# Two graph layers on one core: program order in two stretches, pair projections in another order, setup in smaller pieces

## The chip, the core and the metric

One core of a Trainium2 chip runs the whole program. The time is that of the device, in microseconds (us), from the first to the last instruction of one execution, and the number compared is the median of several executions. Five engines work side by side, each through its own list of instructions in order: TensorE (PE) multiplies matrices, VectorE (DVE) and ScalarE (ACT) work elementwise and can read what TensorE left in its accumulators (PSUM, eight banks of 128 x 512 fp32), GpSimd (POOL) works elementwise on the on-chip memory (SBUF) and issues stores, and SyncE (SP) issues loads. An engine waits where an instruction needs what another has not yet finished. A tile framework puts in these waits, hands out buffers from pools, and may reorder the instructions of an engine by its own estimate of when each will be ready. `keep_in_program_order` takes that freedom from an instruction.

## The reference

Two layers of attention on a graph with 2,708 nodes and 1,024 features, all in fp32 (the biases `bf`, `bg`, `bW` exist but hold zeros):

```python
def _L0_gnn_ref(x, adj, Wf, bf, Wg, bg, W, bW):
    f = x @ Wf + bf
    g = x @ Wg + bg
    e = jax.nn.relu(f @ g.T)
    attention = jax.nn.softmax(jnp.where(adj > 0, e, NEG), axis=1)
    return attention @ (x @ W + bW)

def _L1_gnn_ref(input, adj, W, a1, a2):
    h = input @ W
    e = jax.nn.leaky_relu(h @ a1 + (h @ a2).T, negative_slope=0.2)
    attention = jax.nn.softmax(jnp.where(adj > 0, e, neg), axis=1)
    return jax.nn.relu(attention @ h)

# x: (2708, 1024), adj: (2708, 2708) int32
h = jnp.maximum(_layernorm(x), 0.0)
x = x + _L0_gnn_ref(h, adj, ...)
h = jnp.maximum(_layernorm(x), 0.0)
x = x + _L1_gnn_ref(h, adj, ...)
```

## The kernel before

The kernel works by panels of 512 or a few more columns (p = 0 to 4) and by pairs of 128-row tiles (q = 0 to 9, and one left-over pair, LEFT). Every product of 2 x 2 blocks is made from seven products instead of eight, named M1 to M7; some of the seven accumulate in the same PSUM bank, one after the other, so the bank must have been read in between.

**Stages.** First `M = Wf Wg^T`, by rows, with transposes of `Wf` and `Wg` on TensorE. Then for each panel of layer 0: `project_q` (B = M h), `scores` (h B, mask, running maximum), softmax, `aggregate` (attention times h), `project` (times W, plus x). Layer 1 has only `aggregate` and `project`. The projection of the last panel goes pair by pair (`by_pair`), so that its rows are done early.

**Work handed out behind TensorE.** Small pieces of vector work wait in a list; `behind(us)` is called after each product and spends a credit on them. The loads of the first two entries are issued ahead.

```python
def one():
    for it in later[:2]:
        if it[1]:
            it[1]()
            it[1] = None
    us, _, go = later.pop(0)[:3]
    go()
    return us

def behind(us, psum_free=False):
    credit[0] = min(credit[0] + us, 2 * us)
    while later and credit[0] > 0 and (psum_free or not later[0][3]) and (...):
        credit[0] -= one()
```

**The setup of the pairs.** For each pair of row tiles: load x, layernorm (`norms`), store the rows, transpose them on TensorE (`transposes`, needs a PSUM bank), form the sums of the seven products (`sums`) and store them in `hs_d`, from which `scores` loads them again; and two dot products per tile (`dots`).

```python
put_norms = lambda q: put(4.2, lambda: norms(q), lambda: fetch(q))
put_rows = lambda q: put(0.5, lambda: rows(q))
put_dots = lambda q: put(3.2, lambda: bias(q), ready=lambda: vb[0] is not None)
...
transposed_wg(0, ws)                 # 32 transposes into 8 banks, copied out by DVE and ACT in turn
for a in range(NC):
    ...
        transposed_wf(i)
    half_row_of_M(a, 0)
    ...                              # a == NH: ws = fetch_wg(1); a == NH + 2: transposed_wg(1, ws)
    bias_of_g(a, ws)
    behind(2.0 if a < NH else 5.0, True)
```

**Scores.** TensorE makes seven products per pair; DVE adds and masks them; `make_until(q + 2)` forces the setup of the pairs two ahead.

```python
rate = (0.6, 1.0, 0.65, 0.65, 0.65)[p]
...
nc.hold = True                       # DVE in program order from here
for q in range(NQ):
    make_until(q + 2)
    if q + 2 <= LEFT:
        fetch(q + 2)                 # adjacency for the masks
    ...
    product(q, M1, X, True)          # each loads As <- hs_d, then 4 matmuls
    ...
    behind(rate, True)               # after each product
```

**Projection.** `finish` adds a product to the rows of x and stores them; `join` adds a term that two outputs share.

```python
ws = {m: load_W(l, m) for m in (M1, M2)}
lefts = []
for ta, tb, (a11, a12), (a21, a22) in todo:      # four DVE sums per pair, all pairs first
    s = [slot(f"ps{i}", (P, NH, P)) for i in range(4)]
    add(s[0], a21, a22); sub(s[1], s[0], a11); sub(s[2], a11, a21); sub(s[3], a12, s[1])
    lefts.append({M1: a11, M2: a12, M5: s[0], M6: s[1], M7: s[2], M3: s[3], M4: a22})
...
copy1 = nc.vector.tensor_copy if by_pair and l == 0 else nc.scalar.copy
for group, left in (zip([[t] for t in todo], [[t] for t in lefts]) if by_pair else [(todo, lefts)]):
    for m in (M1, M2, M5, M6, M3, M7, M4):
        which = "x" if m in (M1, M2) else "y" if m in (M5, M3) else "z"      # the PSUM bank
        for i, (ta, tb, _, _) in enumerate(group):
            ...                                   # NH matmuls 128 x 512 into that bank
            if m == M1:
                copy1(t(M1), ps)
            elif m == M2:
                finish(ta, 0, ps)
            ...
            behind(rate)
```

Of the kernel before, what the change touches and what calls it, by code (L numbers as in the profile page):

```python
# [33 lines left out]
class InOrder:  # L34


    class Engine:
        def __init__(self, owner, engine):
            self.owner, self.engine = owner, engine

        def __getattr__(self, name):
            f = getattr(self.engine, name)

            def issue(*a, **k):
                i = f(*a, **k)  # L45
                return self.owner.tc.keep_in_program_order(i) if self.owner.hold else i
            return issue

    def __init__(self, tc):
        self.tc, self.nc, self.hold = tc, tc.nc, False  # L50
        self.vector = self.Engine(self, tc.nc.vector)

# [5 lines left out]
def kernel(  # L58
# [122 lines left out]

    later, credit = [], [0.0]

    def put(us, go, fetch=None, takes_psum=False, ready=None):
        later.append([us, fetch, go, takes_psum, ready])

    def one():
        for it in later[:2]:
            if it[1]:
                it[1]()  # L190
                it[1] = None
# [3 lines that stand above are left out]
# [124 lines left out]
    def make_pairs():  # L319
# [7 lines left out]

        def norms(q):
            for k in range(2):
                normalize(xs[q][k])  # L330

        def rows(q):
# [38 lines left out]

        def dots(q):
            for k, t in enumerate(units[q]):
                c = col_of[t]
                dot(r_[:, c:c + 1], xs[q][k], [vb[e][:, :W] for e in range(2)], c0)
                if t == MONO:
                    nc.gpsimd.dma_start(r_[:NM, HALF:HALF + 1], r_[NM:, c:c + 1])

        def drop(q, what):
            seen.setdefault(q, set()).add(what)  # L380
            if len(seen[q]) == 2:
                xs.pop(q)
# [5 lines left out]

        def bias(q):
            dots(q)  # L390
            drop(q, "dots")

        seen = {}
        put_norms = lambda q: put(4.2, lambda: norms(q), lambda: fetch(q))
        put_rows = lambda q: put(0.5, lambda: rows(q))
        put_dots = lambda q: put(3.2, lambda: bias(q), ready=lambda: vb[0] is not None)
        todo = [0, 1, LEFT] + list(range(2, NQ))
# [92 lines left out]
    later[0][1] = None  # L490
    bfb = row_to_all(bf, wab[0])
    transposed_wg(0, ws)
    for a in range(NC):
        for i in range(2 * a, min(2 * a + 2, NC)):
            if i + 2 < NC:
                rows_of_wf[i + 2] = load_rows(wf, i + 2, "wf")
            transposed_wf(i)
        half_row_of_M(a, 0)
        if a == NH:
            dot(c0, halves(bfb), halves(bgb))  # L500
            vb = [slot(f"vb{g}") for g in range(2)]
            for g in range(2):
                spread(vb[g][:, :W], [v[:, 4 * g + j:4 * g + j + 1] for j in range(4)])
            ws = fetch_wg(1)
        bias_of_g(a, ws)
        if a == NH + 2:
            transposed_wg(1, ws)
        behind(2.0 if a < NH else 5.0, True)
    for k in range(NH):
        for a in (k, k + NH):  # L510
            half_row_of_M(a, 1)
            wfT.pop(a)
            behind(5.5, True)
        left_of_q(k)
# [16 lines left out]

    def accumulate(left, right, K, h, order, then, evict, name, prepare={}, rate=0.0, by_k=False, more={}):

# [3 lines left out]
        for m in order:  # L537
# [4 lines left out]
            for k, d in ([(k, d) for k in range(K) for d in range(NH)] if by_k else  # L542
# [7 lines left out]
                if not by_k and k == K - 1:  # L550
                    evict[m](d, ps[d])
                    behind(rate)
            if by_k:
# [13 lines left out]
    def project_q(p, then={}):  # L567
# [55 lines left out]
        def sides(m):  # L623
            for g in range(2):
# [6 lines left out]
                else:  # L631
# [11 lines left out]
                   {M1: second, M2: fourth, M3: lambda: sides(M3), M7: lambda: sides(M7), M4: lambda: sides(M4)},  # L643
                   rate=1.2 if p == 0 else 1.5)
        return B
# [236 lines left out]
    def project(l, p, G, finish, then={}, by_pair=False, rate=2.0):  # L882
# [10 lines left out]
        start_of, join, finish = finish  # L893
        ws = {m: load_W(l, m) for m in (M1, M2)}
        start_of([t for g in todo for t in g[:2]] + ([other] if other else []))
        lefts = []
        for ta, tb, (a11, a12), (a21, a22) in todo:
            s = [slot(f"ps{i}", (P, NH, P)) for i in range(4)]
            add(s[0], a21, a22)
            sub(s[1], s[0], a11)  # L900
            sub(s[2], a11, a21)
            sub(s[3], a12, s[1])
            lefts.append({M1: a11, M2: a12, M5: s[0], M6: s[1], M7: s[2], M3: s[3], M4: a22})
        acc1 = {}
# [24 lines left out]

        copy1 = nc.vector.tensor_copy if by_pair and l == 0 else nc.scalar.copy  # L930
        for group, left in (zip([[t] for t in todo], [[t] for t in lefts]) if by_pair else [(todo, lefts)]):
            acc, tmp = {}, {}
            for m in (M1, M2, M5, M6, M3, M7, M4):
                start = m in (M1, M5, M6)
                w_ = ws.pop(m) if m in ws else load_W(l, m)
                which = "x" if m in (M1, M2) else "y" if m in (M5, M3) else "z"
                for i, (ta, tb, _, _) in enumerate(group):
# [3 lines left out]
                    for k in range(NH):  # L941
                        nc.tensor.matmul(ps, left[i][m][:, k, :], w_[k], start=(start and k == 0), stop=(k == NH - 1),  # L942
                                         skip_group_check=True)
                    if start:
                        tmp[m, i] = slot(f"pt{m}")
                    t = lambda m: tmp[m, i][:, :W]
                    o = {M3: M6, M7: M5, M4: M1}.get(m)
                    if m == M1:
                        copy1(t(M1), ps)
                    elif m == M2:  # L950
                        finish(ta, 0, ps)
                    elif o is None:
                        add(t(m), ps, t(M1))
                    elif join is None:
                        add(t(o), ps, t(o))
                        finish(tb if m != M3 else ta, 0 if m == M4 else 1, t(o))
                    else:
                        finish(tb if m != M3 else ta, 0 if m == M4 else 1, ps)
                    if join and m == M6:
                        join(tb, 1, t(M5))  # L960
# [5 lines left out]
                if m in then:  # L966
                    then.pop(m)()


# [54 lines left out]
    def scores(p, B):  # L1024
# [8 lines left out]
        S = [None] * NT  # L1033
        rate = (0.6, 1.0, 0.65, 0.65, 0.65)[p]
        lefts = {}
# [32 lines left out]

        nc.hold = True
        left_over = None  # L1070
        for q in range(NQ):
            n = P
            make_until(q + 2)
            if q + 2 <= LEFT:
                fetch(q + 2)
# [66 lines left out]
        behind(rate, True)  # L1142
        nc.hold = False
        return S, acc
# [174 lines left out]
    for p in range(NP):  # L1319
        got["S"], got["acc"] = scores(p, B)  # L1320
        generated[p] = NQ + 1
        S = got["S"]
        hooks = {M1: lambda p=p: take_max(p), M2: lambda p=p: take_softmax(p)}
        if p + 1 < NP:
            B = project_q(p + 1, hooks)
        else:
            project(0, p - 1, G.pop(p - 1), finish0(p - 1), hooks)
            scores_before()
        then = {M5: prepare_W} if p == 0 else {}
# [136 lines left out]
```

## Time and profile before

| | |
|---|---|
| time, median of 3 | 3160.89 us (3159.83 to 3162.55) |
| span of the profiled execution | 3162.6 us |
| PE busy | 3059.7 us, 97% |
| DVE, POOL, ACT busy | 1831.2, 465.2, 443.6 us |
| DMA | 651.83 MB, mean 206 GB/s |
| mean granted TensorE clock | 0.988 |

TensorE works nearly all the time, so it is read by where it does not: the table of stretches (busy time of each engine between two moments, and the TensorE clock granted there), the waits (who waited for whom, how long and how often), and the timeline (instructions of one stretch, with the idle time ahead of them in brackets). In names such as `sx<-B,As` the tile written stands left of the arrow and the tiles read right of it. Every DVE instruction bears the line of one helper, L45, so DVE's work is told apart by tiles.

### The profile page before, as it was taken

What the parts mean: (1) busy time and instruction counts of PE and PEld (TensorE: products, weight loads), DVE (VectorE), ACT (ScalarE), POOL (GpSimd) and SP (SyncE); (2) the same over time, 40 slices, a digit from 0 to 9 for tenths busy, and PEclk for the clock granted to TensorE, in tenths of its full rate; (3) what the DMA queues carried; (4) which work ended last, traced back from release to release, by engine and by line L of the source; (5) the groups of instructions that cost most, each with busy time, mean ns of one, the idle gap of its engine ahead of it and who ended that gap; (6) DMA issues with size and microseconds to landing.
All of it is one profiled execution on the core that took longest, in us unless ns stands there. A gap on an engine that the chain in (4) does not pass through costs nothing.

```text
span 3162.6 us, 36212 instructions
## 1 busy us (share of the span) xinstructions
PE 3059.7 (97%) x12712; PEld 2266.0 (72%) x12712; DVE 1831.2 (58%) x3728; ACT 443.6 (14%) x783; POOL 465.2 (15%) x664
## 2 busy tenths in 40 slices
PE   8998899999999999999999999997999999999998
PEld 5576677667876688876888885864767758678684
DVE  6767686386722687227871468558574471744612
ACT  3411020000200002001020002103131120211200
POOL 3624102110002100033000111020011020120102
PEclk9999999999999999999999999998999999999999
DMA  7878838778447795478945677686655565565655
GB/s 249 298 226 279 285 131 315 218 236 244 148 126 181 220 269 177 144 201 235 289 143 154 181 211 222 215 265 210 201 177 177 153 200 158 172 195 176 212 160 192
DMA packets 379046, 651.83 MB, mean 206 GB/s; under 512 B 170784, under 2 KB 211264, under 8 KB 378864
## 3 DMA queue, kind: packets, MB, share of 16 engines
q1 hardware_dynamic: 335920, 525.38, 55.0%
q0 software_dynamic: 42944, 124.13, 11.7%
q8 instruction: 101, 1.65, 0.2%
q14 instruction: 81, 0.66, 0.1%
HBM read 536.68 MB, written 112.67 MB: 205 GB/s over the span
## 4 chain that ended last, share of the span: by engine, by line
PE 78%; DVE 5%; DMA 3%; issue 3%; SPq 1%; POOL 0%; ACT 0%; DVEq 0%; POOLq 0%; ACTq 0%
PE gz L544 11%; PE gy L544 11%; PE gx L544 11%; PE sz L1046 6%; PE gv L544 5%; PE pz L942 5%; PE px L942 4%; PE py L942 4%; PE sx L1046 4%; PE sy L1046 4%; PE qz L544 3%; PE qy L544 2%; PE qx L544 2%; SPq L139 1%; PE po L915 1%
## 5 line engine op out<-in xcount | busy, mean ns | idle before, releaser
L1046 PE MATMUL sz<-B,As 128*128 128x288 f32 (+2 forms) x1200 | 295.3, 395 | 14.3 <-DVE st L45 10.0
L1046 PEld LDWEIGHTS sz<-B,As 128*128 128x128 f32 x1200 | 228.5, 191 | 66.1 <-DVE st L45 14.5
L850 POOL TENSOR_TENSOR gT<-gT,rr 128x2304 f32<-128x2304 f32 (+5 forms) x20 | 72.7, 3635 | 1113.3 <-DVE rr L45 1009.5
L1046 PE MATMUL sx<-B,As 128*128 128x288 f32 (+2 forms) x800 | 202.2, 396 | 18.5 <-DMA As<-hs_d 16.9
L1046 PE MATMUL sy<-B,As 128*128 128x288 f32 (+2 forms) x800 | 200.1, 393 | 3.0 <-DVE st L45 3.0
L544 PE MATMUL gz<-Sa,hc 128*128 128x288 f32 (+2 forms) x800 | 187.8, 395 | 2.3 <-ACT gT L839 2.3
L1046 PEld LDWEIGHTS sx<-B,As 128*128 128x128 f32 x800 | 152.3, 192 | 51.2 <-DMA As<-hs_d 16.7
L544 PE MATMUL gz<-P,hc 128*128 128x288 f32 (+2 forms) x800 | 186.0, 393 | 2.3 <-ACT gT L839 2.3
L544 PE MATMUL gx<-P,hc 128*128 128x288 f32 (+2 forms) x800 | 185.7, 394 | 0.0
L544 PE MATMUL gy<-T,hc 128*128 128x288 f32 (+2 forms) x800 | 184.2, 391 | 0.0
L544 PEld LDWEIGHTS gz<-Sa,hc 128*128 128x128 f32 x800 | 152.3, 191 | 37.0 <-ACT gT L839 4.8
L1046 PEld LDWEIGHTS sy<-B,As 128*128 128x128 f32 x800 | 152.3, 191 | 34.8 <-DVE st L45 4.3
L544 PEld LDWEIGHTS gz<-P,hc 128*128 128x128 f32 x800 | 150.9, 190 | 35.6 <-ACT gT L839 4.4
L544 PEld LDWEIGHTS gx<-P,hc 128*128 128x128 f32 x800 | 152.9, 191 | 32.7 <-issue 1.9
L544 PEld LDWEIGHTS gy<-T,hc 128*128 128x128 f32 x800 | 152.0, 190 | 30.5
L942 PE MATMUL px<-w,gT 128*128 128x512 f32 x320 | 147.5, 614 | 10.8 <-issue 5.8
L942 PE MATMUL py<-w,ps 128*128 128x512 f32 x320 | 141.9, 593 | 0.0
L942 PE MATMUL pz<-w,ps 128*128 128x512 f32 x320 | 141.7, 593 | 0.0
L143 POOL DMA_DIRECT2D out_dram<-x_res x180 | 89.0, 501 | 266.1 <-DVE x_res L45 230.2
L942 PEld LDWEIGHTS px<-w,gT 128*128 128x128 f32 x320 | 61.6, 196 | 88.3 <-issue 80.8
L45 DVE TENSOR_TENSOR gT<-gy,u 128x288 f32<-128x288 f32 (+2 forms) x40 | 14.8, 432 | 183.5 <-PE gy L809 183.5
L45 DVE TENSOR_TENSOR u<-gz,m 128x288 f32<-128x288 f32 (+2 forms) x40 | 17.6, 439 | 174.6 <-PE gz L544 174.2
(317 smaller groups left out, 5059.8 us busy)
## 6 DMA issues: line engine op xcount, KB each, us to landing
hc<-hg_d SPq DMA_DIRECT2D x350, 512.0 KB, 4.0
As<-hs_d SPq DMA_DIRECT2D x150, 512.0 KB, 5.0
w<-wt_d SPq DMA_DIRECT2D x96, 512.0 KB, 5.3
w<-in_L_gnn_W_dram SPq DMA_DIRECT2D x72, 512.0 KB, 3.8
md<-md_d SPq DMA_DIRECT2D x56, 512.0 KB, 4.6
adj_i<-in_adj_dram SPq DMA_DIRECT2D x200, 128.0 KB, 4.6
hg_d<-g POOLq DMA_DIRECT2D x40, 512.0 KB, 5.2
hs_d<-hsT POOLq DMA_DIRECT2D x40, 512.0 KB, 6.0
```

What stands on the lines that cost most here:

```text
L45: i = f(*a, **k)
L139: tc.keep_in_program_order(nc.sync.dma_start(a, b))
L143: nc.gpsimd.dma_start(a, b)
L544: nc.tensor.matmul(ps[d], left(m, k, d), right(m, k), start=(start and k == 0), stop=(k == K - 1 and m not in more), skip_group_check=True)
L850: nc.gpsimd.tensor_tensor(of(e, s), of(e, s), by(s, k), OP.mult)
L915: nc.tensor.matmul(ps, carry[:, e, k], w_[k], start=(start and k == 0), stop=(k == NH - 1), skip_group_check=True)
L942: nc.tensor.matmul(ps, left[i][m][:, k, :], w_[k], start=(start and k == 0), stop=(k == NH - 1), skip_group_check=True)
L1046: nc.tensor.matmul(ps[:n, :h], lefts[q][:, i % 2, c, :n], B[m][c // 2][:, c % 2, :h], start=(start and c == 0), stop=(c == NH - 1), skip_g ...
```

## The change

It has five parts. (1) While the first two rows of M are made, DVE and ACT keep to program order; before, the framework could move layernorm and dot products ahead of the copies that TensorE waits for. (2) The pairs' setup is cut into smaller pieces (one tile instead of two for norms and dots), the loads of five list entries are issued ahead until the first panel's scores are done, transposes may run behind four of the seven products of the first `project_q`, and the first scores hand out setup at 1.3 instead of 0.6 per product until it is finished. (3) The projection of layer 0's last panel but one keeps DVE in program order. (4) A projection by pairs takes its products in another order, gives M4 a bank of its own (`pv`), forms the four sums of a pair only when the pair before is at M6, and copies M1 by ACT. (5) `InOrder` takes names of engines instead of a flag. The product that lands in M4's bank is complete because the part it shared with the bank of M6 and M7 is now added on DVE after M7.

```diff
-                return self.owner.tc.keep_in_program_order(i) if self.owner.hold else i
+                return self.owner.tc.keep_in_program_order(i) if self.name in self.owner.hold else i
 ...
+    ahead = [5]
 ...
-        for it in later[:2]:
+        for it in later[:ahead[0]]:
 ...
-        put_norms = lambda q: put(4.2, lambda: norms(q), lambda: fetch(q))
+        def put_norms(q):
+            put(2.1, lambda: normalize(xs[q][0]), lambda: fetch(q))
+            put(2.1, lambda: normalize(xs[q][1]))
+
         put_rows = lambda q: put(0.5, lambda: rows(q))
-        put_dots = lambda q: put(3.2, lambda: bias(q), ready=lambda: vb[0] is not None)
+        def put_dots(q):
+            for k in range(2):
+                put(1.6, lambda k=k: bias(q, k), ready=lambda: vb[0] is not None)
 ...
     bfb = row_to_all(bf, wab[0])
+    nc.hold = ("vector", "scalar")
     transposed_wg(0, ws)
 ...
         behind(2.0 if a < NH else 5.0, True)
+        if a == 1:
+            nc.hold = ()
 ...
-                    behind(rate)
+                    behind(rate, m in room)
 ...
-                   rate=1.2 if p == 0 else 1.5)
+                   rate=1.2 if p == 0 else 1.5, room=(M1, M2, M7, M4) if p == 0 else ())
 ...
-        ws = {m: load_W(l, m) for m in (M1, M2)}
+        order = (M1, M5, M2, M6, M7, M3, M4) if by_pair else (M1, M2, M5, M6, M3, M7, M4)
+        ws = {m: load_W(l, m) for m in order[:2]}
 ...
-        copy1 = nc.vector.tensor_copy if by_pair and l == 0 else nc.scalar.copy
-        for group, left in (zip([[t] for t in todo], [[t] for t in lefts]) if by_pair else [(todo, lefts)]):
+        lefts = {0: [left_of(*todo[0])] if by_pair else [left_of(*t) for t in todo]}
+        for j, group in enumerate([[t] for t in todo] if by_pair else [todo]):
             acc, tmp = {}, {}
-            for m in (M1, M2, M5, M6, M3, M7, M4):
-                start = m in (M1, M5, M6)
+            left = lefts.pop(j)
+            for m in order:
+                apart = by_pair and m == M4
+                start = m in (M1, M5, M6) or apart
-                which = "x" if m in (M1, M2) else "y" if m in (M5, M3) else "z"
+                which = "x" if m in (M1, M2) else "y" if m in (M5, M3) else "v" if apart else "z"
 ...
-                        copy1(t(M1), ps)
+                        nc.scalar.copy(t(M1), ps)
 ...
+                    if by_pair and m == M7:
+                        join(tb, 0, ps) if join else add(t(M1), ps, t(M1))
 ...
+                if by_pair and m == M6 and j + 1 < len(todo):
+                    lefts[j + 1] = [left_of(*todo[j + 1])]
 ...
-        rate = (0.6, 1.0, 0.65, 0.65, 0.65)[p]
+        rates = (0.6, 1.0, 0.65, 0.65, 0.65)
 ...
+            rate = 1.3 if NQ - 1 not in made else rates[p]
 ...
         got["S"], got["acc"] = scores(p, B)
         generated[p] = NQ + 1
+        ahead[0] = 2
 ...
+            nc.hold = ("vector",)
             project(0, p - 1, G.pop(p - 1), finish0(p - 1), hooks)
+            nc.hold = ()
```

## The prediction

> **What bounds the kernel now.** I read the page first: TensorE is busy for 3059.7 of 3162.6 us at a mean clock of 0.988, so no change that leaves the products alone can take away more than about 103 us of idle time and 0.012 x 3163 = 38 us of lost clock. Then I asked for the table of stretches, cut where the stages begin and end. The columns are the stretch, its length, busy time (and count) of PE, PE's weight loads, DVE, ACT and POOL, the granted TensorE clock, the DMA share and GB/s.
>
> ```profile
> 0.00:21.50 21.50, 9.31 (x49) 9.10 (x50) 8.88 (x30) 5.08 (x9) 2.33 (x15) 0.78 0.76 241
> 21.50:205.00 183.50, 183.50 (x660) 110.06 (x660) 131.89 (x292) 62.01 (x117) 85.12 (x120) 1.00 0.77 266
> 205.00:395.00 190.00, 164.36 (x711) 125.62 (x711) 138.02 (x287) 21.70 (x40) 49.09 (x63) 0.96 0.86 273
> 1905.00:1963.70 58.70, 52.77 (x130) 23.68 (x128) 55.21 (x108) 20.34 (x33) 4.92 (x9) 0.94 0.72 228
> 2096.70:2180.20 83.50, 60.02 (x136) 26.42 (x132) 52.64 (x128) 10.22 (x17) 11.39 (x19) 0.85 0.88 305
> ```
>
> These are the start, the rest of M with the first projection, the first scores, the last but one projection, and the pair projection of layer 0. They hold 12.2 + 0 + 25.6 + 5.9 + 23.5 = 67.2 us of TensorE's idle time, and most of the lost clock: 0.04 x 190 = 7.6, 0.06 x 58.7 = 3.5 and 0.15 x 83.5 = 12.5 us in the last three. So the change aims at where the loss is. Next the waits of TensorE over the whole run, longest first:
>
> ```profile
> PE sx L1046 <- DMA As<-hs_d: 16.9, 4, 9.0
> PE sz L1046 <- DVE st L45: 10.0, 9, 2.1
> PE pz L942 <- DVE x_res L45: 8.2, 3, 5.5
> PE wT_ps L452 <- DVE wgT L45: 7.8, 1, 7.8
> PE mx_ps L733 <- DVE mx L45: 7.1, 1, 7.1
> PE px L942 <- issue: 5.8, 1, 5.8
> ```
>
> Each is a single long wait or a few: loads of the pairs' transposed sums, DVE reading a bank late, and the copies of the transposed Wg. Last, the timeline of the pair projection, TensorE's rows:
>
> ```profile
> 2096.75 3.70 PE L942 MATMUL px<-w,gT 128*128 128x512 f32 x8
> 2105.43 6.67 PE L942 MATMUL px<-w,gT 128*128 128x512 f32 x8 [4.98 <-DVE pt L45]
> 2111.93 3.60 PE L942 MATMUL py<-w,ps 128*128 128x512 f32 x8
> 2127.11 3.70 PE L942 MATMUL pz<-w,gT 128*128 128x512 f32 x8 [1.28 <-DVE x_res L45]
> 2140.93 5.97 PE L942 MATMUL px<-w,gT 128*128 128x512 f32 x8 [5.83 <-issue]
> 2161.11 3.70 PE L942 MATMUL pz<-w,gT 128*128 128x512 f32 x8 [1.33 <-DVE x_res L45]
> ```
>
> One product of 8 instructions costs 3.43 us start to start (2111.93 to 2115.37 in the same answer). After both waits of about 5 us the next product takes 6.67 and 5.97 us: a long wait is paid twice.
>
> **What the Trainium skill says.** "TensorE: Matmul & The Clock Gate", Part 1, says that an idle window of about 3.4 us halves TensorE's clock and that a busy window of the same length restores it. The trace agrees: product 2105.43 takes 6.67 instead of 3.43 us after 4.98 us of idling, and 3.70 us after waits of 1.3 us. "PSUM — Partial Sum Buffer", The four PSUM rules, says that neither GpSimd nor a DMA can touch PSUM, so each bank above waits for DVE or ACT, and which of them is free decides; in this trace all reads of the banks named here are DVE's or ACT's. "DMA: Bandwidth & Descriptors", Specifications, gives 358 GB/s as a core's share of the memory; the trace shows 408 GB/s over 2105 to 2110 us, so I use its figures from the trace and only keep the warning that 305 GB/s in the pair projection is not far from a limit.
>
> **Part 1, the start.** The 32 transposes of Wg end at 4.43 + 5.82 = 10.25 us. DVE then does dot products on Wf, which wait for a load until 12.03 us, and layernorm of x until 17.4, and only then the four copies (2.43 us at 17.32); TensorE waits 7.76 us. In the changed program's list for DVE the four copies stand first. Copies on DVE and ACT side by side end near 13 us; the transposes of the second Wf tile need its load, which DVE's own use dates to about 14.2; so the first row of M begins near 15.6 instead of 21.48. **Gain 5.5.** The stretch after it had no idle time at all, so this passes on in full. One thing moves the other way: SP now issues the second half of Wg after the 24 loads of the left-over rows. Those waited 23.1 us for a memset on POOL before; now the memset follows the fourth row of M, near 50 us, the 20 small loads take about 10 us, and Wg's landing took 8.3 us in the median, so it lands near 69 to 71. TensorE wants it at 79.7 - 6 = 73 to 74. It should just do; **cost 1**, as an average over none and several.
>
> **Part 2, the first scores.** Loss before: 25.6 idle and 7.6 of clock, 33 us. Most (16.9 + 3.1) is waiting for As, which waits for the stores of pairs made only two ahead, and whose issue stands behind 16 row loads on SP. In the changed list the transposes of two more units run inside the first project_q, the rest of the units within the first three pairs of the scores, and no row loads are left among the loads of later pairs. DVE's work per pair without setup, summed from its rows at 207 to 231 us, is about 10 us; TensorE needs 7 x 1.94 = 13.6. In the first three pairs setup adds 3 sums of four at 2.6, 2 norms at 1.9 and 6 dots at 1.6, 21 us in all: 17 us of DVE per pair against 13.6 + 1.75 (16 transposes) = 15.3 for TensorE, so 5 us of waits on DVE take the place of those on As; I add 2 for the second As load, which now stands behind 16 row loads at the start, and 1 for clock. 33 - 8 = **gain 25**. The added DVE work in project_q (two units, about 20 us) fits: DVE is busy there for 22.3 of 40 us (160 to 200).
>
> **Part 3, the last but one projection.** Loss 5.9 + 3.5 = 9.4 us, nearly all of it one wait of 5.5 us for DVE reading M7's bank. In the new DVE list, from the end of the second product on, 39 instructions stand before that read; back to back they start every 0.605 us (5 in 3.09 us), so 23.6 us, and it comes at about 1945. TensorE ends M7's first product near 1944.3 and wants the bank again at 1947.7. No long wait; DVE stays nearly full, and ACT loads tables more often. **Gain 7.**
>
> **Part 4, the pair projection.** 14 products are 48 us; from 2096.75 to the end near 2164.7 they take 68, so 20 us are lost (4.98 + 1.28 + 5.83 + 1.33 idle, the rest clock and DVE's backlog). M5 now follows M1, so M1's copy has 3.43 us and is on ACT: the two long waits go, with their slow products. M4 has its own bank: two waits of 1.3 go. But M7 now follows M6 directly in one bank, so a DVE read of about 1.3 us stands there: 2 x 1.3 minus what TensorE slips in between, 2 us. The tail after the last product was 15.4 us (layernorm, dots, maximum, transposes). M3 now stands right before M4, so DVE still has the first tile's rows to finish when the second's arrive: their chain took 8 us (2156.4 to 2164.5) and begins 3.4 us before the end instead of 8.4, so the tail grows by about 3. And the same bytes must arrive in less time: about 16 MB of W, rows and stores in 50 us is 320 GB/s, so I take 3.5 us of waiting for W. 20 - 2 - 3 - 3.5 = **gain 11.5**. Layer 1's pair projection had no long wait (0.79 us before its last M4); the new order trades that for waits at M7: **0**.
>
> Sum: 5.5 - 1 + 25 + 7 + 11.5 = 48. I take off 4, since a new order of loads and pools can cost something that I don't see in lists without times: 3161 - 44 = **3117 us**, a ratio of 0.986.
>
> **Rivals.** (a) *DVE becomes the bound in the first scores.* For it: 17 against 15.3 us per pair, and ten waits of TensorE on DVE's st already there. Against it: only three pairs. If DVE falls behind by a pair, with slow clock after each wait, part 2 brings 12 instead of 25: 3130. (b) *The second half of Wg comes late.* DVE has dot products on it in its list between copies that free banks, so a late load stops DVE, then ACT, then TensorE. For it: the issue now depends on POOL's memset. Against it: 3 us of slack by my count. If the load lands at 85, TensorE loses 12: 3129. (c) *The pair projection is bound by its loads.* For it: 305 GB/s already, 400 in single slices. Then 25.5 MB at 340 GB/s take 75 us, and the gain is 8.5, with the longer tail 6: 3122. (d) *All waits go and nothing replaces them*: 6 + 32 + 9 + 17 = 64 us, 3097.
>
> **Range and chances.** The gains are bounded by losses that I can read, so the time should not rise; both (a) and (b) together give about 3142. The range is 3098 to 3138. Faster by over 2% needs 3097.7, which is (d): 0.09. Slower by over 2% would need a new loss of over 60 us, more than any here: 0.01. Within 2%: 0.90.
>
> **What would show it.** In the changed profile: the first row of M begins near 15.6 us and no wait for wgT over 2 us (part 1); no wait for wg over 4 us; in the first scores under 10 us of idle TensorE, with st or Sb as releasers and hardly any As (part 2); no wait over 3 us for x_res in the last but one projection (part 3); no 128x512 product of 6 us in the pair projection, waits of about 1 us at M7's bank, and a last wait for mx of about 10 us (part 4). A wait on As above 10 us, or on w above 5, would prove the step wrong that names it; a time above 3142 would prove the sum wrong.

## The result and the profile after

The changed kernel takes **3147.19 us** (median; 3145.09 to 3148.11) against 3161.37 us (3159.83 to 3162.55) for the kernel before, measured side by side: a ratio of **0.9954**, 95% interval 0.9937 to 0.9972. It is faster, by 14 us; the prediction was 44. The profiled spans are 3162.6 and 3144.7 us, 17.9 apart, and the stretches tell where these come from.

The table of stretches of the changed kernel, cut where the same stages begin and end: start, rest of M, first `project_q`, first scores, last but one projection, pair projection of layer 0. The columns are those of the table in the prediction.

```profile
0.00:15.00 15.00, 7.86 (x48) 7.26 (x49) 5.26 (x20) 4.55 (x8) 2.32 (x15) 1.00 0.80 276
15.00:151.60 136.60, 132.68 (x442) 68.70 (x441) 102.78 (x243) 51.81 (x97) 60.62 (x89) 0.99 0.75 261
151.60:231.20 79.60, 63.89 (x262) 49.57 (x260) 56.37 (x107) 20.45 (x40) 43.48 (x56) 0.89 0.83 280
231.20:399.60 168.40, 155.59 (x678) 120.74 (x678) 111.06 (x243) 11.97 (x23) 27.98 (x39) 0.96 0.87 259
1904.00:1953.70 49.70, 49.70 (x127) 22.50 (x126) 46.08 (x90) 20.62 (x32) 4.91 (x9) 1.00 0.84 266
2086.80:2162.20 75.40, 56.33 (x137) 25.04 (x133) 51.50 (x128) 11.34 (x19) 11.39 (x19) 0.89 0.92 334
```

The prediction had `project_q` and the rest of M in one line; the kernel before, cut at `project_q` alone:

```profile
152.00:207.00 55.00, 55.00 (x230) 42.95 (x228) 34.39 (x55) 6.83 (x15) 18.30 (x27) 1.00 0.73 238
```

TensorE was never idle in it before; now it is idle for 79.6 - 63.9 = 15.7 us and runs at 0.89 of its clock. Stage by stage, from the start of one stage to the start of the next in the two timelines:

| stage | before, us | after, us | gain | predicted |
|---|---|---|---|---|
| start and rest of M, to `project_q` | 151.96 | 151.63 | 0.3 | 4.5 |
| first `project_q` | 55.0 | 79.6 | -24.6 | } 25 |
| first scores | 190.0 | 168.35 | 21.65 | } |
| from there to the last but one projection | 1508.5 | 1504.4 | 4.1 | 0 |
| last but one projection | 58.2 | 49.7 | 8.5 | 7 |
| last aggregation of layer 0 | 133.1 | 133.1 | 0 | 0 |
| pair projection of layer 0 | 83.5 | 75.4 | 8.1 | 11.5 |
| the rest | 982.4 | 982.55 | -0.2 | 0 |

So the two projections did what was expected of them, and start, `project_q` and first scores together lost 2.6 us where 29.5 were to be gained. The scores are nearly as much shorter as predicted; they only begin 24 us later. (Stretches of single executions differ by chance too: in E2 below, whose program is that of the kernel before up to there, `project_q` begins at 149.95 us instead of 151.96, so a difference of 2 us between two of them says nothing.) TensorE's waits of the changed kernel show the same:

```profile
PE sx L1061 <- DMA As<-hs_d: 12.2, 2, 12.0
PE mx_ps L740 <- DVE mx L45: 9.9, 1, 9.9
PE qx L551 <- ACT m L45: 9.7, 1, 9.7
...
PE h_ps L336 <- ACT M L45: 5.1, 1, 5.1
...
PE wT_ps L455 <- DMA wf<-in_L_gnn_Wf_dram: 4.9, 5, 2.6
PE py L953 <- DMA w<-in_L_gnn_W_dram: 4.7, 1, 4.7
```

The waits for `wgT` (7.8), `x_res` (8.2) and of `px` (5.0 and 5.8) are gone, but for 0.7 us of `px`. New are those for `m` and `M` in `project_q`, where TensorE waits for ACT to copy a PSUM bank out, those for Wf at the start, and one for W. One long wait for As has stayed, 12.0 us.

In the pair projection, the timeline of TensorE:

```profile
2101.75 3.70 PE L953 MATMUL pz<-w,ps 128*128 128x512 f32 x8 [0.78 <-DVE pt L45]
...
2131.69 1.99 PE L953 MATMUL py<-w,ps 128*128 128x512 f32 x2 [4.75 <-DMA w<-in_L_gnn_W_dram]
2133.48 4.44 PE L953 MATMUL pz<-w,ps 128*128 128x512 f32 x8
```

The long waits behind M1 are gone, M7's bank costs 0.78 us, and one load of W comes 4.75 us late; the two instructions after it take 1.99 us instead of 1.02 in the kernel before, and the next product 4.44 instead of 3.60. SyncE's waits and its timeline tell why the load is late:

```profile
SPq L139 <- DMA hg_d<-g: 15.8, 2, 14.2
```

```profile
2107.20 5.47 SPq L139 DMA_DIRECT2D w<-wt_d  x4
2126.92 2.40 SPq L139 DMA_DIRECT2D w<-in_L_gnn_W_dram  x2
```

Before it could issue this load, SyncE waited 14.2 us until a store of `g`, the sums of a pair's rows for layer 1, had landed: W, `g`, `hsT`, As and the adjacency take their buffers from one pool of twelve. The last wait, for `mx`, is 9.9 us in the list above, 2.8 longer than before.

### The profile page after: what moved, and what is told of

It reads as the page before. It is cut to its first block, busy times and chain, and to the rows that moved or that the text cites. A ratio compares the mean times of both kernels' runs of the same rounds, so it can differ in the third digit from the quotient of the medians.

```text
span 3144.7 us, 36222 instructions
## 1 busy us (share of the span) xinstructions
PE 3053.0 (97%) x12712; PEld 2263.8 (72%) x12712; DVE 1827.6 (58%) x3730; ACT 447.0 (14%) x788; POOL 462.8 (15%) x664
## 3 DMA queue, kind: packets, MB, share of 16 engines
q0 software_dynamic: 42944, 124.13, 11.8%
## 4 chain that ended last, share of the span: by engine, by line
PE 83%; DMA 5%; issue 4%; DVE 4%; POOL 2%; SPq 1%; ACT 0%; POOLq 0%; DVEq 0%; ACTq 0%
PE gz L551 12%; PE gy L551 12%; PE gx L551 11%; PE sz L1061 7%; PE gv L551 5%; PE pz L953 5%; PE sy L1061 4%; PE sx L1061 4%; PE px L953 4%; PE py L953 4%; PE qz L551 3%; PE qy L551 2%; PE qx L551 2%; PE M_ps L467 2%; SPq L139 1%
## 5 line engine op out<-in xcount | busy, mean ns | idle before, releaser
L1061 PEld LDWEIGHTS sz<-B,As 128*128 128x128 f32 x1200 | 227.7, 190 | 58.2 <-DVE st L45 11.9
L1061 PEld LDWEIGHTS sx<-B,As 128*128 128x128 f32 x800 | 152.3, 191 | 45.4 <-DMA As<-hs_d 13.1
L953 PEld LDWEIGHTS py<-w,ps 128*128 128x128 f32 x320 | 60.5, 191 | 81.1 <-issue 77.5
```

The lines of the kernel that those rows point to most:

```text
L1061: nc.tensor.matmul(ps[:n, :h], lefts[q][:, i % 2, c, :n], B[m][c // 2][:, c % 2, :h], start=(start and c == 0), stop=(c == NH - 1), skip_g ...
```

## The experiments

Three theories of the late scores stood at the start. A: transposes behind the products of `project_q` take PSUM banks that ACT frees late. B: smaller pieces and the look-ahead of five move loads and layernorm. C: program order at the start pushed the rows of x back. All times are medians, compared with the kernel before on the same chip (3160.8 to 3162.1 us there).

| | kernel | us | ratio, 95% interval |
|---|---|---|---|
| E1 | change without transposes in `project_q` | 3158.1 | 0.9989 (0.9982 to 0.9996) |
| E2 | before + the two projections | 3144.5 | 0.9947 (0.9930 to 0.9964) |
| E3 | before + program order at the start | 3161.0 | 1.0000 (0.9992 to 1.0009) |
| E4 | change, look-ahead of two | 3132.6 | 0.9909 (0.9895 to 0.9924) |
| E5 | change, two while M is made, then five | 3135.4 | 0.9920 (0.9905 to 0.9934) |
| E6 | E4 without program order at the start | 3134.8 | 0.9921 (0.9904 to 0.9937) |
| E7 | E4, sums ahead of dot products | 3132.8 | 0.9911 (0.9897 to 0.9926) |
| E8 | E4, ACT in program order in `project_q` | 3139.6 | 0.9932 (0.9917 to 0.9947) |
| E9 | E4, adjacency loaded later | 3127.1 | 0.9888 (0.9873 to 0.9902) |
| E10 | change, left-over rows not ahead | 3139.3 | 0.9924 (0.9909 to 0.9939) |
| E11 | E4, g on DVE | 3125.7 | 0.9882 (0.9867 to 0.9896) |
| E12 | E4, rate 0.6 in the first scores | 3129.1 | 0.9891 (0.9875 to 0.9908) |
| E13 | change, g on DVE | 3129.5 | 0.9900 (0.9885 to 0.9914) |
| E14 | E9 and E11 together | 3125.1 | 0.9884 (0.9868 to 0.9900) |
| E15 | E14, rate 0.6 | 3114.8 | 0.9854 (0.9840 to 0.9869) |
| E16 | before, g on DVE | 3153.6 | 0.9976 (0.9967 to 0.9984) |

### E1 to E4: which part makes the scores late

E1, transposes not allowed in `project_q`:

```diff
-                   rate=1.2 if p == 0 else 1.5, room=(M1, M2, M7, M4) if p == 0 else ())
+                   rate=1.2 if p == 0 else 1.5, room=())
```

> The changed kernel without transposes behind the products of the first project_q; all else of the change stays. Theory A (the transposes take the PSUM banks there, and ACT's list has layernorm ahead of the copies that free them): no wait of TensorE above 3 us between 150 us and the first score; the scores begin near 208 us instead of 231.2; but fewer pairs are ready then, so waits for As of 10 to 25 us come back in the first scores, and the total is 3135 to 3150 us. Theory B (the smaller pieces and the look-ahead of five bring layernorm and row loads to the front of ACT's and SP's lists, with or without transposes): the waits in project_q stay, the scores begin after 220 us, and the total is 3150 or more. Theory C (the start: holding program order pushed x's rows back): scores begin after 220 us here as well.

Measured: 3158.1 us. The scores begin at 214.8 us, waits of 5.6 us for `m` stay in `project_q`, and waits for As of 27 us in all come back. Theory A fits in part. Without the transposes `project_q` takes 63.5 us instead of 79.6, so 12.6 us of its loss hang on them beyond their own 3.5. But one wait of 5.4 us stays, and the scores take 194.4 us instead of 168.4: in all the kernel is 11 us slower without the transposes than with them. They are the useful piece of part 2.

E2, the two projections alone on the kernel before (`hold` around `project(0, p - 1, ...)`, and the whole new body of `project`):

> The kernel before with the two projections of the change alone (vector work in program order in the last but one, the new order, the bank of M4 and the sums pair by pair in the last); start and setup as before. If the gains of the two projections are what the stretches of the changed kernel show (8.5 and 8.1 us), the time is 16 to 17 us below the kernel before, 3144 to 3146, about that of the whole change, and start and setup together then bring nothing or a little less than nothing. If instead some of those gains hang on the setup, it is above 3150.

Measured: 3144.5 us, 16.9 below the kernel before. Parts 3 and 4 account for all that the change brought; start and setup together bring nothing. In this run's trace the two stretches take 49.7 and 77.1 us, which is 8.5 and 6.4 less than before; the load of W is 5.4 us late here too.

E3, the start alone on the kernel before:

```diff
+    nc.hold = ("vector", "scalar")
     transposed_wg(0, ws)
 ...
+        if a == 1:
+            nc.hold = ()
```

> The kernel before with program order of DVE and ACT during the first two rows of M, and nothing else. My prediction's step: the first row of M begins near 15 us and the lead of 5.5 us lasts to the end: 3155.5 us. Rival (the lead is eaten by waits for rows of Wf and by half clock on the first rows, as the stretch after shows): the first row begins near 15 us, but row 3 is at most 2.5 us earlier than before and the time is within 2 us of the kernel before, 3159 to 3163. Theory C for the late scores: the scores begin 5 us or more later than 207 us here too.

Measured: 3161.0 us, a ratio of 1.000. The first row of M begins at 14.07 us instead of 21.48, but the third at 38.27 instead of 39.21, and the scores at 206.06. In place of the wait for `wgT` stand five waits for rows of Wf, 6.1 us. The rival holds, and theory C falls.

E4, the look-ahead alone taken back:

```diff
-    ahead = [5]
+    ahead = [2]
```

> The changed kernel with loads issued two list entries ahead, as before the change, instead of five; smaller pieces and transposes in project_q stay. Theory A (transposes and banks): the stall in project_q stays within 5 us of the changed kernel's, scores begin at 226 us or later, and the total is 3145 to 3155. Theory B (look-ahead puts row loads in front): the stall shrinks to under 8 us in all, scores begin before 217 us and the total is 3130 to 3140.

Measured: 3132.6 us; the scores begin at 215.06, and in `project_q` 4.2 + 0.9 us of waits are left of 15.7. Theory B holds for the look-ahead: five entries instead of two cost 14.6 us, all that the transposes bring and more.

### E5, E6 and E10: where the look-ahead does its harm

E5, `ahead[0] = 5` only from the first `project_q` on:

> The changed kernel with loads two list entries ahead while M is made, and five from the first project_q to the end of the first scores. Theory S (the look-ahead of five does its harm at the start: SyncE's list gets x's rows, above all the left-over rows that wait for GpSimd's memset and rows that wait for buffers of the first pairs, in front of Wf, Wg and the rows that layernorm needs next, and the setup runs behind from there on): within 3 us of the kernel with two throughout, 3130 to 3136, scores begin near 215 us. Theory Q (it does its harm in project_q and the scores, where rows of x stand in front of As and the adjacency): near the changed kernel, 3142 to 3148, with scores beginning after 225 us or a longer wait for As.

Measured: 3135.4 us, scores from 219.5. Of the 14.6 us, 11.8 arise while M is made: theory S, with a rest for Q. The new wait in `project_q` is 8.0 us for a copy of `hsT`.

E6, the two-entry kernel without the start:

> The changed kernel with loads two entries ahead, and without program order of DVE and ACT in the first two rows of M. If the start alone brings nothing, as its run on top of the kernel before showed (ratio 1.000), and its lead is lost in any setup: within 2 us of the kernel with two entries ahead, 3131 to 3135. If the lead of about 3.5 us with which that kernel reached project_q (148.2 us against 152.0 before) is the start's, the time is 3 to 4 us longer, 3135 to 3137.

Measured: 3134.8 us (3132.23 to 3140.37). That is 2.2 us more than E4, but within the spread of the runs (E4: 3132.12 to 3135.63), so a worth of program order at the start is not shown here either. With two entries ahead, two loads of Wf stand before 16 row loads that precede them in the changed kernel's list, and the third row of M begins at 35.48 us in E4 instead of 36.98; but in E5, the same program up to there, it begins at 37.45, so this is not clear of chance.

E10, the look-ahead of five, without the left-over pair's rows:

```diff
-            if it[1]:
+            if it[1] and (i < 2 or not it[5]):      # it[5]: rows of the left-over pair
```

> The changed kernel with its look-ahead of five, except that the left-over pair's rows (which wait for GpSimd's memset) are loaded only when they are next or next but one in the list, as before the change. In SyncE's list nothing else moves, but the second half of Wg comes ahead of these 24 loads again. Theory S1 (these rows at the head of SyncE's queue are what costs): near the kernel with two entries ahead, 3131 to 3136, scores begin at 214 to 220 us. Theory S2 (it is the look-ahead of the other pairs' rows, whose buffers come free only with the first pairs' dot products, that holds the queue for 16 us from 67 to 83 us): near the changed kernel, 3143 to 3148.

Measured: 3139.3 us, scores from 220.7. It lies between S1 and S2: these loads (20 in the timeline), which stand behind a memset that GpSimd reaches only at 54 us, make about 8 of the 14.6 us; the rest stays with the other pairs' rows.

### E8, E11, E13 and E16: how late loads become TensorE's waits

E8, ACT in program order (`nc.hold = ("scalar",)` around the first `project_q`):

> The changed kernel with loads two entries ahead, and ACT in program order in the first project_q, so that the copies of M1's products out of their banks are not behind layernorm's square root. Theory A' (ACT's list with layernorm ahead of the copies makes the 4.2 us wait there): the wait of qx for the copies m vanishes, scores begin at 208 to 211 us instead of 215.1, and the time is 3126 to 3130. Rival (DVE's backlog alone: whatever the order, the chain of sums, layernorm and sides of project_q is what is late): the wait moves to another instruction and the scores begin within 3 us of 215.

Measured: 3139.6 us; the wait for `m` grows to 11.6 us, and the scores begin at 220.9. But the program's own order does not put the copies ahead: the root `rs` (at 165.16) and the two activations of x (167.52) stand before the copies of `m` (168.94), where in E4 a copy came right after the root (165.56). So E8 does not test theory A', and no run here keeps the copies ahead of the root. What its trace shows is that the root itself is late: ACT waits 8.3 us for `mv`, which DVE delivers. So the question was why DVE is late. The changed kernel's timeline with all engines, at the wait of 5.13 us, has the answer:

```profile
151.80 0.68 DVE L45 SCALAR_TENSOR_TENSOR junk<-x,vb 128x512 bf16<-128x512 f32 x1
...
152.59 4.41 DVE L45 SCALAR_TENSOR_TENSOR junk<-x,vb 128x512 bf16<-128x512 f32 x1
152.73 1.28 POOL L303 TENSOR_TENSOR g<-x 128x512 f32<-128x512 f32 x1
...
153.96 1.27 POOL L305 TENSOR_TENSOR g<-x 128x512 f32<-128x512 f32 x1
155.18 1.26 POOL L304 TENSOR_TENSOR g<-g,x 128x512 f32<-128x512 f32 x1
156.39 0.56 POOL L143 DMA_DIRECT2D hg_d<-x  x1
...
156.94 0.68 DVE L45 BATCH_NORM_STATS2 bn<-x 128x6 f32<-128x512 f32 x1
...
158.19 0.20 DVE L45 BATCH_NORM_AGGREGATE mv<-bn 128x2 f32<-128x12 f32 x1
158.48 0.29 ACT L45 ACTIVATE rs<-mv,eps 128x1 f32<-128x1 f32 x1 [8.43 <-DVE mv L45]
158.68 0.56 ACT L45 COPY M<-M_ps 128x512 f32<-128x512 f32 x1
...
159.30 1.12 PE L336 MATMUL h_ps<-ident,x 128*128 128x128 f32 x4 [5.13 <-ACT M L45]
```

Read from below: TensorE waits for ACT's copy of M, which stands behind the root `rs`; `rs` waits for DVE's `mv`; and DVE stood for 4.41 us in an instruction that takes 0.68 us just before, while GpSimd did three sums `g` without a pause. Twenty us later the same happens to `hT<-hT,hT`, 4.47 us at 172.33 instead of 1.36, with GpSimd's next three sums at 171.86 to 175.58; after it comes the wait of 9.71 us for `m`. E11 puts the four sums on DVE:

```diff
-        on = nc.vector if l else nc.gpsimd
+        on = nc.vector
```

> The changed kernel with loads two entries ahead, and the four sums of a pair's rows (g) in layer 0 on DVE instead of GpSimd: 4 x 0.69 = 2.8 us of DVE more per pair, 28 us in all. If DVE's stretched instructions (4.47 us for one that takes 1.36 otherwise, 1.6 to 1.7 for 0.69) come from GpSimd's elementwise work at the same time, none of the DVE instructions in the first project_q takes over twice its usual time. Time: if DVE is the bound of project_q and of the first three pairs of the scores, 3135 to 3142; if buffers held by g are (theory H), 3126 to 3132.

Measured: 3125.7 us, just below the better of the two expectations, and no DVE instruction in `project_q` takes over twice its usual time. (The sums also end earlier on DVE, so the buffers of `g` may come free earlier: the time holds both effects, DVE's rows only the first.) The same DVE instruction in the kernel with GpSimd's sums (E4, first) and without them (E11, second):

```profile
160.68 4.47 DVE L45 TENSOR_TENSOR hT<-hT,hT 128x1152 f32<-128x1152 f32 x1
```

```profile
157.46 1.34 DVE L45 TENSOR_TENSOR hT<-hT,hT 128x1152 f32<-128x1152 f32 x1
```

`project_q`, E4 first and E11 second, in the table of stretches:

```profile
148.20:215.10 66.90, 61.78 (x263) 47.89 (x261) 47.77 (x94) 18.83 (x37) 37.95 (x51) 0.95 0.87 300
```

```profile
149.80:208.30 58.50, 58.50 (x262) 46.37 (x260) 44.75 (x98) 16.45 (x32) 17.27 (x30) 1.00 0.90 304
```

58.5 us is the 55.0 of before and 32 transposes (3.5 us): nothing is lost any more. The work of DVE in the two stretches is not quite the same: in E11 it does nine sums `g` there, and four sums of `hsT` fewer. With four more instructions in all it is busy for 3.0 us *less*.

E13, the same edit on the change as it is:

> The changed kernel as it is (look-ahead of five), with the four sums of a pair's rows (g) in layer 0 on DVE instead of GpSimd. Theory G (late loads only cost because they move layernorm and dot products beside GpSimd's sums, which stretch DVE's instructions to 4.4 us in the chain that frees TensorE's banks): no wait above 3 us in project_q, scores begin at 208 to 214 us, time 3126 to 3132, as with two entries ahead and the sums on DVE. Theory L (the lateness of the loads is enough): waits of 5 us or more stay in project_q, scores begin after 217 us, time 3134 to 3142.

Measured: 3129.5 us, 17.7 less than the change. That is theory G's time. Its places fit only in part: `project_q` takes 61.9 us with one wait of 3.1, but begins at 154.4 (rows of Wf are waited for, 6.7 us), so the scores begin at 216.3. With the sums on DVE the look-ahead of five still costs 3.8 us (E13 against E11); the rest of the 14.6 needs the collisions.

E16, the same edit on the kernel before:

> The kernel before the change, with nothing but the four sums of a pair's rows in layer 0 on DVE. TensorE had no wait in its project_q, so only the first scores can gain, where DVE's instructions took 3.1 and 4.1 us for 0.76 beside GpSimd's sums: 3157 to 3161. If the cost of GpSimd's sums is paid in the kernel before as well (theory G without the change's crowding): 3150 to 3156. If DVE's extra 2.8 us per pair cost more than they save: above 3163.

Measured: 3153.6 us, 7.2 less than before. GpSimd's sums cost the kernel before too, in its first scores (190.0 to 181.6 us). The change moved more of them into `project_q`, where DVE's chain ends at TensorE's banks.

### E7, E9, E12, E14 and E15: what is left in the first scores

E7, each pair's sums ahead of its dot products:

```diff
-            if i > 1:
-                put_dots(q)
             put(2.7 if q != LEFT else 0.0, lambda q=q: last(q))
+            if i > 1:
+                put_dots(q)
```

> The changed kernel with loads two entries ahead, and in the setup list each pair's sums (and their store, from which As is loaded) ahead of its four dot products instead of behind them. Theory D (the wait of 11.7 us for As in the first scores is DVE's backlog: in program order the third pair's sums came at 249.8 to 252.4 us, behind dot products of 1.6 us each): the sums come 3 us or more earlier, the wait for As falls to under 8 us and the time to 3127 to 3130. Rival (the wait is bound by the row loads or by the stores' issue on GpSimd): the wait stays at 10 us or more and the time within 2 us of 3132.6.

Measured: 3132.8 us; theory D falls. The sums do come 6.3 us earlier (243.5 to 246.1 us), but the wait for As grows to 14.2. I had also taken the wrong sums for the third pair's: by TensorE's timeline of E4 eight of the eleven units are transposed before the scores begin, the third pair at 108.65 us, and the last of its four stores is issued at 118.1. Its data had long been there. SyncE's waits from 225 to 262 us and its timeline in E7 tell what was missing:

```profile
SPq L139 <- DMA hg_d<-g: 17.7, 2, 16.3
```

```profile
244.75 4.67 SPq L139 DMA_DIRECT2D adj_i<-in_adj_dram  x4
249.47 5.37 SPq L139 DMA_DIRECT2D adj_t<-in_adj_dram  x4
255.15 2.23 SPq L139 DMA_DIRECT2D As<-hs_d  x4
```

The adjacency goes into a buffer that `g` holds until its store has landed: SyncE waits 16.3 us for it. It issues in order, so the loads of As stand behind these eight until 255.15. In E4 it is alike: SyncE waits 8.5 us for a store of `hsT` and then 9.2 for one of `g`, and As is issued at 251.49. E9 moves the adjacency back:

```diff
-            if q + 2 <= LEFT:
+            if p and q + 2 <= LEFT:
                 fetch(q + 2)
 ...
             product(q, M7, Z, False)
+            if not p and q + 2 <= LEFT:
+                fetch(q + 2)
```

> The changed kernel with loads two list entries ahead; in the first scores the adjacency of the pair two ahead is loaded after the product M7 of a pair instead of before its M1, so that it stands behind three of the four As loads in SyncE's list. Theory H (the wait of about 12 us for As is head-of-line blocking: in the kernel with sums ahead of dot products As of the third pair was stored by 246.9 us, but issued only at 255.2, behind eight adjacency loads whose buffer was held by g and its store, 16.3 us): the wait for As falls under 6 us, the first scores end 6 to 10 us earlier than 383.8, time 3123 to 3127. Rival D2 (DVE's backlog makes As late; in the kernel with two entries ahead the third pair's sums come at 249.8 to 252.4 whatever SyncE does): the wait stays 9 us or more and the time within 2 us of 3132.6.

Measured: 3127.1 us; the longest wait for As falls from 11.7 to 7.0, not under 6. The first scores end at 380.2 us, 3.6 earlier and not 6 to 10. Rival D2 falls, and theory H holds in part, with a second half that I had not named (and the data that its text calls the third pair's are the ninth's): As now is first in the queue and waits for the same buffers itself, 4.3 us for a store of `g` by SyncE's waits from 240 to 247 us. GpSimd makes these `g` from 236.46 on and issues their stores at 242.03; As follows at 245.41.

E12, the old rate of handing out (`rate = rates[p]`, 0.6 in the first panel):

> The changed kernel with loads two entries ahead, and the first scores handing out setup at 0.6 per product as before the change instead of 1.3. If the early finish of the setup is what shortens the scores (my prediction's step): scores begin near 215 us as with 1.3, but several waits for As of 3 to 9 us come back, 10 to 16 us in all, and the time is 3140 to 3148. If the room for transposes in project_q alone brings the gain: within 3 us of 3132.6.

Measured: 3129.1 us, 3.5 less than with 1.3; I had expected 8 to 15 more. Waits for As come, but 9.8 us in all instead of 13.1. The early finish of the setup is not what shortens the scores; they take 167.3 us here, 168.7 in E4, and 194.4 where `project_q` has no room for transposes (E1).

E14, E9 and E11 together:

> Two entries ahead, the pairs' sums on DVE, and in the first scores the adjacency loaded after M7; rate 1.3. If the two remedies are independent (5.5 and 7 us): 3119 to 3122. If both remove the same wait (the buffers that g and its store hold): 3124 to 3127, no better than the sums on DVE alone.

Measured: 3125.1 us, no better than E11. That both remedies free the same buffers is not shown by this: the waits for As do fall further, from 11.4 us in E11 to 7.3, and in the scores a wait for DVE takes the place of what they lose:

```profile
PE sx L1061 <- DMA As<-hs_d: 6.5, 2, 5.6
PE sy L1061 <- DVE st L45: 6.1, 1, 6.1
```

E15, the same at 0.6:

> The same with the first scores handing out setup at 0.6 per product. If a high rate makes DVE the bound in the first three pairs, as the gain of 3.5 us at 0.6 suggested: 2 to 4 us less than the same kernel at 1.3. If that gain came only from spreading GpSimd's sums: the same within 1.5 us, or longer.

Measured: 3114.8 us, 10.3 less than E14, and 32 less than the change. It is the fastest kernel here. Its first scores, and all waits of TensorE in its first 400 us:

```profile
207.50:365.10 157.60, 154.31 (x677) 120.29 (x677) 115.25 (x253) 11.98 (x23) 17.53 (x31) 0.99 0.95 283
```

```profile
PE wT_ps L455 <- DMA wf<-in_L_gnn_Wf_dram: 4.7, 4, 3.2
PE wT_ps L431 <- DMA wg<-in_L_gnn_Wg_dram: 4.5, 1, 4.5
PE sz L1061 <- DMA As<-hs_d: 2.4, 1, 2.4
PE sx L1061 <- DMA As<-hs_d: 0.9, 1, 0.9
```

I read this so: at 1.3 the setup of three pairs is pressed into the first pairs' products and DVE cannot keep up (E14's wait for `st`, gone here); at 0.6 it has the time. With GpSimd's sums and the adjacency ahead of As the lower rate gained 3.5 us (E12), with both moved 10.3; which of the two makes the difference was not tried.

## Why the prediction was wrong

**The step that failed** is part 2's "The added DVE work in project_q (two units, about 20 us) fits: DVE is busy there for 22.3 of 40 us". By busy time it does fit: DVE was busy for 34.4 of 55 us before and 56.4 of 79.6 after. But busy time is not work. In the changed kernel 3.7 + 3.1 + 0.9 us of DVE's busy time there is standing beside GpSimd's sums, in the chain layernorm, root, ACT's copies, PSUM banks. The kernel before had the sign within the 40 us that I counted, beside three sums of GpSimd from 162.69 to 166.41 us:

```profile
162.71 4.33 DVE L45 TENSOR_TENSOR hT<-hT,qT 128x576 f32<-128x576 f32 x1
```

This instruction takes 0.75 us in the changed kernel (at 180.59). It cost TensorE nothing before, since no wait of TensorE hung on it; the change brings more of GpSimd's work there (busy for 43.5 us instead of 18.3), more of DVE's, and transposes that wait for the banks at the end of that chain.

`project_q` lost 24.6 us: 15.7 idle, 3.5 for the transposes moved there, and 5.4 of slow clock. Of the idle time the timeline shows these 7.7 us directly; that most of the rest goes with the sums too, E13 shows (one wait of 3.1 us is left), but not by which steps: DVE then works through its list back to back, and ACT keeps the root ahead of its copies, which no run changed. None of my rivals had it: (a) looked at DVE in the scores. The runs show it by taking GpSimd's sums away (E13: 17.7 us less, E11: nothing lost in `project_q`), and show that the look-ahead of five moved the work there (E4: 14.6 us less). Together (E11) they bring 21.5 us and not 32.3, so 10.8 us are one loss that either remedy takes away.

**The Trainium skill** has the mechanism, which my prediction left out because the change edits no line of GpSimd's: "SBUF — State Buffer", section "SBUF: two separate sides", says that DVE and GpSimd share one pair of ports under an exclusive lock, and that a DVE operation with two inputs in SBUF blocks in full while a GpSimd operation that reads SBUF has it. The trace agrees: 4.41 and 4.47 us instead of 0.69 and 1.36, and 1.34 with the sums on DVE. But the page gives the ports for one whole instruction, to the engine that starts first; here three sums in a row kept them, and DVE's instruction had, by the profile, begun at 152.59, before the first sum at 152.73. The measurement decides. "GPSIMD Engine Reference", 4.1 Engine selection, puts elementwise work on VectorE and calls GpSimd about half as fast for two inputs; here one sum takes 1.26 to 1.28 us there and 0.69 on DVE.

**Part 1** (5.5, less 1 for Wg). The step itself came as read: first row at 15.00, no wait for `wgT`, none for the second half of Wg, so rival (b) fell. "The stretch after it had no idle time at all, so this passes on in full" was wrong: it had none because its loads had been given 6 us more. Once TensorE is early, it waits for rows of Wf behind 16 row loads. E3: 0.0 us.

**Part 2, the scores** (25): 21.65 in the stretch itself. The wait for As of 12 us, where I had said "hardly any", is not one for data: adjacency loads ahead of As in SyncE's queue, and then As itself, wait for buffers that `g` holds (E7, E9). In the changed kernel SyncE waits 13.1 us for a store of `hsT` and then 10.7 for one of `g` before the adjacency goes out at 261.19 and As at 267.56. My sign for a wrong step, "a wait on As above 10 us", came true. Rival (a), DVE as the bound, was hidden behind it and came out in E14.

**Part 3** (7): 8.5, with no wait left. **Part 4** (11.5): 8.1. Of the terms of the sum, the tail was right (3; the wait for `mx` grew by 2.8), M7's bank took 0.78 instead of 2, and the "3.5 us of waiting for W" was too small: 4.75 idle, and about 1.8 us more for the slow instructions after it. Rival (c), bound by the loads in all, did not come about: there is one such wait at 334 GB/s, and that load was issued late, behind a buffer that `g` held for 14.2 us. No run takes this wait away. E2 confirms parts 3 and 4 together, 16.9 us.

**The 4 us taken off** for losses not seen were of the wrong size and sign: the long stretch between gained 4.1 by scattered waits, which no run here explains. The time is also above the 3142 us that, by my own sign, prove the sum wrong.

## What to carry to other kernels

Free time on an engine is no room for work by itself: ask what the engine next to it will do at the same time, and whether the added work stands in a chain that frees a buffer. A single long duration of an instruction whose others are short (4.4 beside 0.69) is the sign to look at the other engines' rows in the same microseconds. And a longer look-ahead on a queue that issues in order is a reordering: whatever waits at its head holds all behind it, as the left-over rows and the adjacency did here.

## What the runs showed of the hardware

DVE stood still not for one GpSimd instruction but for a whole row of them: 4.41 us from 152.59, over three sums of 1.28, 1.27 and 1.26 us, until GpSimd turned to issuing a store at 156.39. In E4 and the changed kernel the `hT` instruction of 1.36 us took 4.47, again over three sums. So four sums on GpSimd (5.1 us of its time) can cost DVE more than doing them itself (4 x 0.69 = 2.8): in E4 those from 160.21 us on cost it 3.1 + 0.9 = 4.0 us. Not every DVE instruction stands: the three stretched ones named above read two tiles of SBUF, while `u<-qz,m`, which reads one of them from PSUM, took its usual 0.46 us at 199.93 beside the changed kernel's sums from 197.06 to 202.13. I had not expected that taking work from an engine can slow it down.
